# Storing only the read parts of a depthwise convolution, with its partitions regrouped as (q/k/v, chunk, channel), and loading the constants from GpSimd's queue

## The chip, the cores and the metric

The kernel runs on one core of one Trainium2 chip. The metric is the device time of one execution in microseconds (us). The kernel before was run three times: 3765.82, 3767.5 and 3774.27 us, median 3767.5 us.

## The reference

The input x is one image of 48 channels, 256 x 256, float32. Two layers are added to it in turn, each behind a group normalisation (16 groups of 3 channels):

```
x = x + L0(gn(x))        # attention between 4x4 patches
x = x + L1(gn(x))        # 64x64 windows: sum over 3 of (C, H, W) matrix products
```

Layer 0 is what the change touches. Its core is

```
qkv = depthwise3x3(einsum('bchw,oc->bohw', x, w_qkv))     # 144 channels = 3 x 8 heads x 6
q, k, v = heads(unfold(split(qkv, 3)))                    # per head 96 rows (6 channels x 16 pixels of a patch)
q, k = q / |q|, k / |k|                                   # over the 96 rows
out = v @ softmax(q^T k * temperature)                    # 8 heads, patches against patches
out = einsum(fold(out), w_proj)
```

There are 64 x 64 = 4096 patches inside the image (a border of zero patches is handled by a constant). The products of logits are made at nearly full float32 precision from two halves: q and k are split into a high part `oh` (float32r) and a low part `ol` (the difference), while v is used as it is.

## The kernel before, in words

The program has five stages that follow one another, each with its own loops.

**Statistics.** x is loaded into SBUF in ten parts of rows, the upper half of the image on SP's queue and the lower half on ScalarE's (L424), and VectorE makes statistics of each part (L428). Then come two tiny matmuls and the scaling of the weights `wq` and `wr` (L429 to L438). Before x, in program order, stand the constants: `gm`, `wq`, `wr`, `wp` and the temperatures `tb` are issued by ScalarE's queue (L86, L99, L103, L111), and the 21 pieces of the depthwise weights `dwt` by SP's (L109). The reductions of the temperatures (L115 to L120) end in `large`, an integer that says whether some temperature is so big that the softmax needs its row maxima.

**Pointwise, heads 0 and 1.** 64 products of the 1x1 convolution (L158), with results stored to DRAM in `t1` (L475).

**Depthwise, head 0** (`depthwise_first`, L365 to L406). A head's 18 channels (6 of q, 6 of k, 6 of v) are cut into 7 overlapping chunks of image rows, so that 126 partitions work at once. In the kernel before a partition is (chunk, q/k/v, channel). Ten steps r = 0 to 9 cover the rows of a chunk, four image rows at a time. Each step loads `pad` (L214 for the first two, L216 else), makes nine taps (on TensorE for even r and for r = 9, else on ScalarE and VectorE), squares and sums (L250, L254), norms with a matmul against `same` (L258), a scale (L284), and the split into `oh` (L293) and `ol` (L297). Then all 126 partitions of `o`, `oh` and `ol` are stored (L302) to `qkv[h]`, a DRAM tensor of [3 parts, 7 chunks, 18 x 16 rows, columns]. Of part 0 (`oh`) and part 1 (`ol`) only the rows of q and k are ever read, and of part 2 (`o`) only those of v. In head 0 SP stores `oh` and most `o`, and GpSimd most `ol`.

**Attention** (L521 to L715), under an order written out by hand. A branch on `large` (L487) stands before it. For each of 8 heads there are 16 steps g of two blocks of 128 queries: `scores` makes the logits (48 matmuls a step, L344) and exponentials (L563), `weigh` multiplies by the values (L592). Woven into head h are the depthwise rows of head h+1 (one a step, `rows[g]`), with `pad` loaded on SP's queue one step ahead (L700; for row 0 at the start of the head, L675) and stored on GpSimd's queue (L660, L689). Woven into head 0 alone are the 64 strips of the pointwise convolution of heads 2 to 7 (four a step): a load of x (L179), two products (L185), an eviction by ScalarE (L188), two stores (L197), all DMAs on SP's queue. SP issues in order, so its loads of keys, queries and values (L318) stand in one line with the strips and with `pad`.

**Projection and layer 1** (L719 to L916). The change does not touch these.

The order of the first three stages is a scheduler's: instructions are emitted in program order and moved ahead by priority where their waits allow it. In the stage of the head-0 depthwise only TensorE's order is fixed by hand.

Of the kernel before, what the change touches and what calls it, by code (L numbers as in the profile page):

```python
# [8 lines left out]
F32 = mybir.dt.float32  # L9
F32R = mybir.dt.float32r  # L10
AF = mybir.ActivationFunctionType
ALU = mybir.AluOpType
AX = mybir.AxisListType
# [7 lines left out]
KS = 4  # L21
KK = KS * KS
NH = 8
HD = C * KK // NH
# [3 lines left out]
TMAX = 60.0  # L28
CH = 7
CR = 9  # L30
HC = 3 * C // NH
NP1 = CH * HC
PX = W // KS
H0 = 2
M0 = H0 * HC
# [9 lines left out]
def conv_preact_kernel(  # L45
# [15 lines left out]
    nc = tc.nc  # L61
# [3 lines left out]
    const = ctx.enter_context(tc.tile_pool(name="const", bufs=1))  # L65
    dram = ctx.enter_context(tc.tile_pool(name="dram", bufs=1, space=DRAM))
# [5 lines left out]
    TR = 2 * CR * KS + (CH - 1) * CR * KS  # L72
    CN = CR * PX
    t1 = [dram.tile([(h1 - h0) * HC, TR, W + 2], F32, name=f"t1_{h0}") for h0, h1 in GROUPS]
    qkv = [dram.tile([3, CH, HC * KK, CN + PX], F32, name=f"qkv{h}") for h in range(NH)]

    os_ = dram.tile([NT // TP, C * KK, TP], F32, name="os_")
    x1s = dram.tile([C, H, W], F32, name="x1s")
# [3 lines left out]
    make_identity(nc, ident)  # L82
    ones = const.tile([C, 128], F32, name="ones")
    nc.vector.memset(ones, 1.0)
    gm = const.tile([P2, P2], F32, name="gm")
    nc.scalar.dma_start(out=gm, in_=gmat)  # L86

# [3 lines left out]
    wp = const.tile([P2, P2], F32, name="wp")  # L93
    nc.vector.memset(wp, 0.0)
    for s in range(2):
        r = slice(s * C, (s + 1) * C)
        for h in range(NH if s == 0 else H0):
            o = s * M0 + h * HC if h < H0 else (h - H0) * HC
            nc.scalar.dma_start(  # L99
                out=(wq[r] if h < H0 else wr[0:C])[:, o : o + HC].rearrange("c (z e) -> c z e", z=3),  # L100
                in_=w_qkvT.rearrange("c (z h e) -> h c z e", z=3, h=NH)[h],
            )
        nc.scalar.dma_start(out=wp[r, r], in_=w_projT)  # L103
    dwt = const.tile([NP1, NH, 9], F32, name="dwt")
    dws = w_dw.rearrange("(z h e) i a b -> z e h (i a b)", z=3, h=NH)
    for z in range(3):
        for j in range(CH):
            p = j * HC + z * 6
            nc.sync.dma_start(out=dwt[p : p + 6], in_=dws[z])  # L109
    tb = const.tile([1, NH], F32, name="tb")  # L110
    nc.scalar.dma_start(out=tb, in_=temp.rearrange("h a b -> (a b) h"))  # L111


    tabs = const.tile([1, 2], F32, name="tabs")
    nc.vector.tensor_reduce(tabs[:, 0:1], tb, AX.X, ALU.max)  # L115
    nc.vector.tensor_reduce(tabs[:, 1:2], tb, AX.X, ALU.min, negate=True)
    tlarge = const.tile([1, 1], F32, name="tlarge")
    nc.vector.tensor_reduce(tlarge, tabs, AX.X, ALU.max)
    large = const.tile([1, 1], mybir.dt.int32, name="large")
    nc.vector.tensor_single_scalar(large, tlarge, TMAX, ALU.is_gt)  # L120
    nmx = const.tile([128, NH * NT // 128], F32, name="nmx")
    nc.vector.memset(nmx, 0.0)

# [5 lines left out]

    same = const.tile([NP1, NP1], F32, name="same")  # L130

    nmul = const.tile([NP1, NH], F32, name="nmul")
    nadd = const.tile([NP1, 1], F32, name="nadd")

# [35 lines left out]
    class Strip:  # L170
# [5 lines left out]
        def load(self):  # L176
            self.xs = cv.tile([64 + C, 2, W], F32, name="xs", bufs=3)
            for s, rows in enumerate(both_halves(xc, 2 * self.j, 2)):
                nc.sync.dma_start(out=self.xs[s * 64 : s * 64 + C], in_=rows)  # L179
# [19 lines left out]
    class Depthwise:  # L199
# [3 lines left out]
            self.h, self.r = h, r  # L203
            self.pool, self.bufs = (pool, 4) if pool else (cv, 1)

        def load(self, engs=None):
            g = [i for i, (h0, h1) in enumerate(GROUPS) if h0 <= self.h < h1][0]
            c0 = (self.h - GROUPS[g][0]) * HC
            self.pad = self.pool.tile([NP1, KS + 2, W + 2], F32, name="pad", bufs=2 * self.bufs)
            rows = t1[g][c0 : c0 + HC, self.r * KS : self.r * KS + CH * CR * KS, :]  # L210
            rows = rows.rearrange("c (j y) x -> j c y x", j=CH)[:, :, : KS + 2, :]
            if engs:
                for j in range(CH):
                    engs[j % len(engs)].dma_start(out=self.pad[j * HC : (j + 1) * HC], in_=rows[j])  # L214
            else:
                nc.sync.dma_start(out=self.pad, in_=rows)  # L216

        def first(self):
            self.acc = self.pool.tile([NP1, KS, W], F32, name="acc", bufs=2)
            nc.scalar.mul(self.acc, self.pad[:, 0:KS, 0:W], dwt[:, self.h, 0:1])  # L220
# [31 lines left out]
        def reduce(self):  # L252
            self.ss = self.pool.tile([NP1, PX], F32, name="ss", bufs=self.bufs)
            nc.vector.tensor_reduce(self.ss, self.sq.rearrange("p a (x b) -> p x a b", b=KS), AX.XY, ALU.add)  # L254

        def norm(self):
            self.pn = one.tile([NP1, PX], F32, name="pn", tag="one")
            nc.tensor.matmul(self.pn, lhsT=same, rhs=self.ss, start=True, stop=True)  # L258

        def root(self, on_scalar=False):  # L260
            n = self.pool.tile([NP1, PX], F32, name="n", bufs=2)
            nc.vector.tensor_scalar_max(n, self.pn, 1e-24)
# [36 lines left out]
        def store(self, parts=(0, 1, 2), eng=nc.gpsimd):  # L299
            px = slice(self.r * PX, (self.r + 1) * PX)  # L300
            for i in parts:
                eng.dma_start(  # L302
                    out=qkv[self.h][i].rearrange("j (c k) n -> (j c) k n", k=KK)[:, :, px],
                    in_=self.o if i == 2 else (self.ol if i else self.oh).bitcast(F32),
                )


# [13 lines left out]

    def load_keys(kt, h, m, eng=nc.sync):
        col = m * 512, (m + 1) * 512
        k0, k1 = (qkv[h][i, :, HD : 2 * HD] for i in range(2))
        to = kt.bitcast(F32)
        load(to[0:HD, 0, :], k0, *col, eng)
        load(to[HD:128, 0, :], k1[:, 0:32], *col, eng)
        load(to[0:64, 1, :], k1[:, 32:], *col, eng)
        load(to[64:128, 1, :], k1[:, 32:], *col, eng)

    def load_queries(qt, h, g):
        col = g * 256, (g + 1) * 256
        to = qt.bitcast(F32)
        for i in range(2):
            qi = qkv[h][i, :, 0:HD]
            load(to[0:HD, i, :], qi, *col)
            load(to[HD:128, i, :], qi[:, 0:32], *col)
            load(to[i * 64 : (i + 1) * 64, 2, :], qi[:, 32:], *col)
# [70 lines left out]
    with tc.tile_pool(name="xn", bufs=1) as xnp, tc.tile_pool(name="cst", bufs=1) as cst, tc.tile_pool(  # L409
        name="nps", bufs=2, space=PSUM  # L410
# [9 lines left out]
        for i, LR in enumerate(parts):  # L420
            j = sum(parts[:i])
            for s in range(2):
                eng = nc.sync if s == 0 else nc.scalar
                eng.dma_start(  # L424
                    out=xr[s * C : (s + 1) * C, j : j + LR, :], in_=xc[:, s * HALF + j : s * HALF + j + LR, :]
# [8 lines left out]
        for g, (w, k) in enumerate(((wq, P2), (wr, C))):  # L434
            m = w.shape[1]
            pb = nps.tile([128, 1], F32, name="pb0", tag="pstat")
            nc.tensor.matmul(pb[:m], lhsT=w[:k], rhs=mean0[:k], start=True, stop=True)
            nc.vector.tensor_scalar_mul(bias[:m, g : g + 1], pb[:m], -1.0)  # L438

        pick = cst.tile([2 * CH, NP1], F32, name="pick")  # L440
        nc.vector.memset(pick, 0.0)
        nc.vector.tensor_copy(
            pick.rearrange("k (j z c) -> k j z c", j=CH, z=3)[:, :, 0:2],
            ident[: 2 * CH, : 2 * CH]
            .rearrange("k (j z u) -> k j z u", j=CH, u=1)
            .to_broadcast([2 * CH, CH, 2, 6]),
        )
        pk = nps.tile([NP1, NP1], F32, name="pk", bufs=1)
        nc.tensor.matmul(pk, lhsT=pick, rhs=pick, start=True, stop=True)
        nc.vector.tensor_copy(same, pk)  # L450
        row = cst.tile([1, NH + 1, NP1], F32, name="row")
        rv = row.rearrange("u i (j z c) -> u i j z c", j=CH, z=3)
        nc.vector.memset(row, 0.0)
        for i in range(NH):
            nc.vector.tensor_copy(
                rv[:, i, :, 0, :], tb[:, i : i + 1].rearrange("u (j c) -> u j c", j=1).to_broadcast([1, CH, 6])
            )
        nc.vector.memset(rv[:, :NH, :, 1, :], 1.0)
        nc.vector.memset(rv[:, NH, :, 2, :], 1.0)
        pr = nps.tile([NP1, NH + 1], F32, name="pr", bufs=1)  # L460
        for i in range(NH + 1):
            nc.tensor.matmul(pr[:, i : i + 1], lhsT=row[:, i, :], rhs=ones[0:1, 0:1], start=True, stop=True)
# [24 lines left out]
    with tc.If(nc.values_load(large) > 0):  # L487
# [8 lines left out]
        with tc.tile_pool(name="mk", bufs=NM) as mk, tc.tile_pool(name="mq", bufs=2) as mq, tc.tile_pool(  # L496
            name="mps", bufs=2, space=PSUM
        ) as mps:
            for h in range(NH):
# [5 lines left out]
                for nb in range(NB):  # L505
# [12 lines left out]
                    b = h * NB + nb  # L518
                    nc.vector.tensor_reduce(nmx[:, b : b + 1], mx, AX.X, ALU.max, negate=True)

    with tc.tile_pool(name="ahead", bufs=2) as ah, tc.tile_pool(name="ae", bufs=3) as ae, tc.tile_pool(  # L521
        name="asm", bufs=6
# [14 lines left out]
        def load_value(h, m):  # L537

            vt = ah.tile([HD, 4 * 128], F32, name="vt")
            load(vt, qkv[h][2, :, 2 * HD :], m * 512, (m + 1) * 512)  # L540
            values[h, m] = vt

        def turn(h, m):
# [88 lines left out]
        with tc.manual_schedule():  # L632
            load_query(0, 1)
            block = scores(0, 0)
            for h in range(NH):
                more = h + 1 < NH
                rows = {r: Depthwise(h + 1, r) for r in range(CR + 1)} if more else {}
                for g in range(NG):
                    p, d, n = rows.get(g - 2), rows.get(g - 1), rows.get(g)
# [82 lines left out]
    with tc.tile_pool(name="pj", bufs=3) as pj, tc.tile_pool(name="pjs", bufs=1) as pjs, tc.tile_pool(  # L722
        name="pps", bufs=3, space=PSUM
# [3 lines left out]
        for t in range(HALF // RP):  # L727
            ot = pj.tile([P2, KK, NP], F32, name="pot")
            xt = pj.tile([P2, RP, W], F32, name="pxt")
            for s in range(2):  # L730
                r = slice(s * C, (s + 1) * C)
# [38 lines left out]
        for s in range(2):  # L770
            nc.scalar.dma_start(
                out=csn[s * 64 : s * 64 + C].rearrange("c (t d) -> c t d", t=T3), in_=Cs.rearrange("t c d -> c t d")
            )
            r = slice(s * 64, s * 64 + C)
# [9 lines left out]
    with tc.tile_pool(name="lx", bufs=3) as lx, tc.tile_pool(name="lz", bufs=2) as lz, tc.tile_pool(  # L784
        name="lr", bufs=2
    ) as lr, tc.tile_pool(name="ly", bufs=4) as ly, tc.tile_pool(name="ps1", bufs=2, space=PSUM) as ps1, tc.tile_pool(
        name="ps2", bufs=2, space=PSUM
# [4 lines left out]
        for s in range(2):  # L792
            r = slice(s * WS, (s + 1) * WS)
# [164 lines left out]
```

## Time and profile before

| what | value |
|---|---|
| runs of the kernel, median (lowest to highest) | 3767.5 us (3765.82 to 3774.27) |
| profiled execution, its own time | 3774.41 us |
| span of the profile | 3772.6 us |
| PE busy / VectorE / ScalarE / GpSimd | 3521.1 / 2185.9 / 1715.5 / 597.5 us |
| largest groups: logits L344, values L592 | 1438.9 and 1423.5 us of PE |
| DMA moved | 441.64 MB, mean 117 GB/s |
| stores of the depthwise results (`qkv`) | 220 issues listed, 504.0 KB each |
| loads of `pad` | 78 issues listed, 761.9 KB each |

In the views of a profile, L12 is line 12 of the kernel, and a group is written as line, engine, operation, output<-input, shape and count. An engine's letter q (SPq, POOLq) is its sequencer, which issues DMAs: a line of SPq with a duration is time that SP spends in issuing. In a table of windows each engine has its busy time and, in brackets, its number of instructions; the last three columns are the granted TensorE clock, the mean busy share of the 16 DMA engines, and GB/s.

In time the stages lie as follows: statistics until 82 us, pointwise until 141 us, depthwise of head 0 with its stores until 286 us, the loading of the first keys until 310 us, attention until about 3320 us, and the rest until 3772.6 us.

### The profile page before, as it was taken

Reading aid. Unit: us, or ns where it says so; the run is one execution under the profiler, and the core shown is the slowest. Engines: PE = TensorE matmul, PEld = TensorE weight load, DVE = VectorE, ACT = ScalarE, POOL = GpSimd, SP = SyncE. Lnnn points to the kernel's source line nnn. Section 1 sums busy time; section 2 is a strip of 40 time slices with the busy share of each in tenths; the row PEclk is TensorE's granted clock in tenths of the full one; section 3 lists DMA queues with packets and bytes.
Section 4 is the critical chain, followed back from the end, with each engine's and each line's share of the span. In section 5 each row is a group of like instructions: output and inputs, shape, how many; then the busy total and the mean of one; then the engine's idle time right before and its main releaser. Section 6 shows DMA issues by size and latency. Waiting matters only on the chain.

```text
span 3772.6 us, 100069 instructions
## 1 busy us (share of the span) xinstructions
PE 3521.1 (93%) x44252; PEld 2916.8 (77%) x44252; DVE 2185.9 (58%) x3514; ACT 1715.5 (45%) x2667; POOL 597.5 (16%) x593
## 2 busy tenths in 40 slices
PE   1877999999999999999999999999999999955998
PEld 0335777788888888888888888888888888812776
DVE  5463675169727962896299439934992222256664
ACT  0224565555545554555455445545554444300222
POOL 0031121012301220122122112211221100010011
PEclk9988999999999999999999999999999999966999
DMA  6575666534433542354245424542543100199784
GB/s 144 170 172 159 178 192 177 166 111 118 114 83 99 126 113 73 104 125 107 84 106 122 101 77 113 119 104 75 125 114 93 46 19 23 31 242 199 128 145 91
DMA packets 307826, 441.64 MB, mean 117 GB/s; under 512 B 98474, under 2 KB 232954, under 8 KB 303160
## 3 DMA queue, kind: packets, MB, share of 16 engines
q1 hardware_dynamic: 253668, 269.65, 27.7%
q0 software_dynamic: 48320, 156.61, 18.5%
q10 hardware_dynamic: 5396, 8.88, 1.1%
q8 instruction: 351, 5.75, 0.7%
q14 instruction: 91, 0.75, 0.1%
HBM read 234.76 MB, written 199.95 MB: 115 GB/s over the span
## 4 chain that ended last, share of the span: by engine, by line
PE 84%; DMA 5%; issue 2%; ACT 0%; SPq 0%; DVE 0%; POOL 0%; ACTq 0%; POOLq 0%
PE big L344 37%; PE big L592 36%; PE pb L856 4%; PE pa L834 2%; PE pc L873 2%; PE big L185 2%; DMA x1s<-pxt 1%; DMA pxt<-in_x_dram 1%; DMA t<-ot 1%; PE pt L609 1%; PE pst L546 1%; PE pn L258 1%; DMA kt<-qkv 0%; DMA os__70<-oo 0%; DMA lxq<-x1s 0%
## 5 line engine op out<-in xcount | busy, mean ns | idle before, releaser
L563 ACT ACTIVATE e<-big,nmx 128x1024 f32<-128x1024 f32 x1024 | 1143.9, 1118 | 833.8 <-PE big L344 622.4
L344 PE MATMUL big<-kt,qt 128*128 128x512 f32 x6144 | 1438.9, 393 | 44.4 <-DMA qt<-qkv 31.6
L592 PEld LDWEIGHTS big<-vn,e 128*64 128x64 f32 x32768 | 1365.8, 137 | 83.4 <-ACT e L563 45.1
L592 PE MATMUL big<-vn,e 128*64 128x96 f32 x32768 | 1423.5, 247 | 5.0 <-ACT ot L188 3.1
L344 PEld LDWEIGHTS big<-kt,qt 128*128 128x128 f32 x6144 | 1145.1, 188 | 307.6 <-issue 46.2
L603 DVE TENSOR_TENSOR oacc<-big,oacc 128x768 f32<-128x768 f32 x480 | 458.1, 954 | 708.5 <-PE big L592 708.5
L239 DVE SCALAR_TENSOR_TENSOR acc<-pad,dwt,acc 126x1024 f32<-126x1024 f32 x592 | 766.2, 1295 | 39.1 <-ACT acc L220 23.5
L297 POOL TENSOR_TENSOR ol<-o,oh 126x1024 fp32r<-126x1024 f32 x78 | 187.1, 2399 | 925.3 <-DVE ss L254 800.9
L576 DVE TENSOR_REDUCE zt<-zs 128x1 f32<-128x4 f32 x256 | 38.9, 152 | 360.4 <-ACT e L563 360.4
L563 ACT ACTIVATION_READ_ACCUMULATOR e<-big,nmx 128x1 f32 x1024 | 196.2, 192 | 0.0
L841 DVE TENSOR_TENSOR lzt<-pa,cbias 128x864 f32<-128x864 f32 (+1 forms) x88 | 137.0, 1628 | 96.9 <-PE pa L834 96.9
L863 ACT COPY lyt<-pb 128x512 f32<-128x512 f32 x144 | 84.5, 586 | 212.9 <-PE pb L856 212.9
L302 POOL DMA_DIRECT2D qkv<-o x72 | 88.6, 1230 | 517.6 <-DVE zu L578 248.9
L613 POOL DMA_DIRECT2D os__70<-oo x128 | 65.2, 515 | 599.6 <-ACT oo L611 598.9
L250 ACT ACTIVATE sq<-acc 126x1024 f32<-126x1024 f32 x74 | 78.2, 1057 | 156.3 <-issue 111.1
L284 DVE TENSOR_TENSOR o<-acc,y 126x1024 f32<-126x1024 f32 x74 | 147.6, 1995 | 0.0
L856 PEld LDWEIGHTS pb<-wsb,lzt 128*64 128x64 f32 x2304 | 125.8, 138 | 27.6 <-issue 19.5
L856 PE MATMUL pb<-wsb,lzt 128*64 128x128 f32 x2304 | 141.7, 279 | 1.3 <-issue 1.3
L188 ACT ACTIVATE ot<-big,bias 108x1024 f32<-108x1024 f32 x64 | 71.1, 1112 | 153.7 <-PE big L185 81.4
L739 PE MATMUL pps<-pot,wp 96*96 96x512 f32 x128 | 78.2, 779 | 58.9 <-DMA pot<-os__70 58.9
L220 ACT ACTIVATE acc<-pad,dwt 126x1024 f32<-126x1024 f32 x74 | 84.1, 1137 | 83.0 <-DMA pad<-t 83.0
L318 POOL DMA_DIRECT2D kt<-qkv x44 | 22.9, 527 | 575.8 <-PE big L344 554.5
(116 smaller groups left out, 1904.5 us busy)
## 6 DMA issues: line engine op xcount, KB each, us to landing
pad<-t SPq DMA_DIRECT2D x78, 761.9 KB
qkv<-ol POOLq DMA_DIRECT2D x78, 504.0 KB, 8.9
qkv<-o POOLq DMA_DIRECT2D x72, 504.0 KB, 6.9
qkv<-oh POOLq DMA_DIRECT2D x70, 504.0 KB, 7.4
t<-ot SPq DMA_DIRECT2D x128, 217.7 KB
qt<-qkv SPq DMA_DIRECT2D x176, 96.0 KB
xs<-in_x_dram SPq DMA_DIRECT2D x128, 96.0 KB
os__70<-oo POOLq DMA_DIRECT2D x128, 96.0 KB, 2.1
```

The costliest lines, as they stand in the source:

```text
L220: nc.scalar.mul(self.acc, self.pad[:, 0:KS, 0:W], dwt[:, self.h, 0:1])
L239: nc.vector.scalar_tensor_tensor(self.acc, self.pad[:, dy : dy + KS, dx : dx + W], dwt[:, self.h, tap : tap + 1], self.acc, ALU.mult, ALU.add,
L284: nc.vector.tensor_tensor(self.o.rearrange("p (a b) x -> p a b x", a=KS), self.acc.rearrange("p a (x b) -> p a b x", b=KS), self.y.rearran ...
L297: eng.tensor_sub(self.ol, self.o, self.oh.bitcast(F32))
L302: eng.dma_start(out=qkv[self.h][i].rearrange("j (c k) n -> (j c) k n", k=KK)[:, :, px], in_=self.o if i == 2 else (self.ol if i else self. ...
L344: nc.tensor.matmul(ps[:, i, :], lhsT=qt[:, r, q0 : q0 + 128], rhs=kts[2 * j + i][:, r // 2, :], start=(r == 0), stop=(r == 2),)
L563: nc.scalar.activation(e[:, j * 1024 : (j + 1) * 1024], ps.rearrange("p a b -> p (a b)"), AF.Exp, bias=nmx[:, b : b + 1], accum_out=zs[:, ...
L592: nc.tensor.matmul(ps[p : p + 64, j // 4, j % 4 * HD : (j % 4 + 1) * HD], lhsT=e[:, mb * 128 + p : mb * 128 + p + 64], rhs=vn, start=(i == 0),
L603: nc.vector.tensor_add(oaccs[h, k], ps[:, :, : 4 * HD], oaccs[h, k])
L841: nc.vector.tensor_tensor(zv[:, :, y0 : y0 + n, :], pa[:, :, : n * T3 * C].rearrange("p s (y k) -> p s y k", y=n), cbias.rearrange("p (u v ...
L856: nc.tensor.matmul(pb[s * WS : (s + 1) * WS, i, :], lhsT=zts[u][:, t * C + c + i, :], rhs=wsb[:, t, :], start=True, stop=True,)
L863: nc.scalar.copy(yt[:, t, :], pb.rearrange("p i x -> p (i x)"))
```

## The change

Five edits:

1. A partition of the depthwise stage is now (q/k/v, chunk, channel): q fills partitions 0 to 41, k 42 to 83 and v 84 to 125. `dwt`, `pick` and `row` are laid out to match. `qkv[h]` becomes [3 parts, 3 (q, k, v), 7 chunks, 96 rows, columns], and the loads of keys, queries and values index it so; their lengths are the same.
2. `store` writes partitions 0 to 83 of `oh` and `ol`, and 84 to 125 of `o`, in place of all 126 of each.
3. `pad` is loaded with three DMAs of 42 partitions in place of one of 126 (or of seven of 18, for the first two rows of head 0).
4. All constants are issued from GpSimd's queue, the temperatures first. SP's and ScalarE's queues begin with x.
5. The reductions that end in `large` are moved in program order behind the statistics of x.

```diff
+NZ = NP1 // 3
...
-    qkv = [dram.tile([3, CH, HC * KK, CN + PX], F32, name=f"qkv{h}") for h in range(NH)]
+    qkv = [dram.tile([3, 3, CH, HD, CN + PX], F32, name=f"qkv{h}") for h in range(NH)]
...
+    tb = const.tile([1, NH], F32, name="tb")
+    nc.gpsimd.dma_start(out=tb, in_=temp.rearrange("h a b -> (a b) h"))
     gm = const.tile([P2, P2], F32, name="gm")
-    nc.scalar.dma_start(out=gm, in_=gmat)
+    nc.gpsimd.dma_start(out=gm, in_=gmat)
...
-            nc.scalar.dma_start(
+            nc.gpsimd.dma_start(
                 out=(wq[r] if h < H0 else wr[0:C])[:, o : o + HC].rearrange("c (z e) -> c z e", z=3),
                 in_=w_qkvT.rearrange("c (z h e) -> h c z e", z=3, h=NH)[h],
             )
-        nc.scalar.dma_start(out=wp[r, r], in_=w_projT)
+        nc.gpsimd.dma_start(out=wp[r, r], in_=w_projT)
...
     for z in range(3):
         for j in range(CH):
-            p = j * HC + z * 6
-            nc.sync.dma_start(out=dwt[p : p + 6], in_=dws[z])
-    tb = const.tile([1, NH], F32, name="tb")
-    nc.scalar.dma_start(out=tb, in_=temp.rearrange("h a b -> (a b) h"))
-
-
-    tabs = const.tile([1, 2], F32, name="tabs")
...
-    nc.vector.tensor_single_scalar(large, tlarge, TMAX, ALU.is_gt)
+            p = (z * CH + j) * 6
+            nc.gpsimd.dma_start(out=dwt[p : p + 6], in_=dws[z])
...
-        def load(self, engs=None):
+        def load(self, engs=(nc.sync,)):
...
-            rows = rows.rearrange("c (j y) x -> j c y x", j=CH)[:, :, : KS + 2, :]
-            if engs:
-                for j in range(CH):
-                    engs[j % len(engs)].dma_start(out=self.pad[j * HC : (j + 1) * HC], in_=rows[j])
-            else:
-                nc.sync.dma_start(out=self.pad, in_=rows)
+            rows = rows.rearrange("(z c) (j y) x -> z j c y x", z=3, j=CH)[:, :, :, : KS + 2, :]
+            for z in range(3):
+                engs[z % len(engs)].dma_start(out=self.pad[z * NZ : (z + 1) * NZ], in_=rows[z])
...
             for i in parts:
+                p = slice(2 * NZ, NP1) if i == 2 else slice(0, 2 * NZ)
                 eng.dma_start(
-                    out=qkv[self.h][i].rearrange("j (c k) n -> (j c) k n", k=KK)[:, :, px],
-                    in_=self.o if i == 2 else (self.ol if i else self.oh).bitcast(F32),
+                    out=qkv[self.h][i].rearrange("z j (c k) n -> (z j c) k n", k=KK)[p, :, px],
+                    in_=(self.o if i == 2 else (self.ol if i else self.oh).bitcast(F32))[p],
                 )
...
-        k0, k1 = (qkv[h][i, :, HD : 2 * HD] for i in range(2))
+        k0, k1 = (qkv[h][i, 1] for i in range(2))
...
-            qi = qkv[h][i, :, 0:HD]
+            qi = qkv[h][i, 0]
...
+        tabs = const.tile([1, 2], F32, name="tabs")
+        nc.vector.tensor_reduce(tabs[:, 0:1], tb, AX.X, ALU.max)
...
+        nc.vector.tensor_single_scalar(large, tlarge, TMAX, ALU.is_gt)
         pick = cst.tile([2 * CH, NP1], F32, name="pick")
...
-            pick.rearrange("k (j z c) -> k j z c", j=CH, z=3)[:, :, 0:2],
+            pick.rearrange("k (z j c) -> k z j c", j=CH, z=3)[:, 0:2],
...
-            load(vt, qkv[h][2, :, 2 * HD :], m * 512, (m + 1) * 512)
+            load(vt, qkv[h][2, 2], m * 512, (m + 1) * 512)
```

More of the change, by code (lines that the diff above doesn't have):

```diff
@@ L107, in conv_preact_kernel @@
         for j in range(CH):
-            p = j * HC + z * 6
-            nc.sync.dma_start(out=dwt[p : p + 6], in_=dws[z])
-    tb = const.tile([1, NH], F32, name="tb")
-    nc.scalar.dma_start(out=tb, in_=temp.rearrange("h a b -> (a b) h"))
-    tabs = const.tile([1, 2], F32, name="tabs")
[L115 to L119, printed above, removed]
-    nc.vector.tensor_single_scalar(large, tlarge, TMAX, ALU.is_gt)
+            p = (z * CH + j) * 6
+            nc.gpsimd.dma_start(out=dwt[p : p + 6], in_=dws[z])
     nmx = const.tile([128, NH * NT // 128], F32, name="nmx")
@@ L438, in conv_preact_kernel @@
             nc.vector.tensor_scalar_mul(bias[:m, g : g + 1], pb[:m], -1.0)
+        tabs = const.tile([1, 2], F32, name="tabs")
+        nc.vector.tensor_reduce(tabs[:, 0:1], tb, AX.X, ALU.max)
+        nc.vector.tensor_reduce(tabs[:, 1:2], tb, AX.X, ALU.min, negate=True)
+        tlarge = const.tile([1, 1], F32, name="tlarge")
+        nc.vector.tensor_reduce(tlarge, tabs, AX.X, ALU.max)
+        large = const.tile([1, 1], mybir.dt.int32, name="large")
+        nc.vector.tensor_single_scalar(large, tlarge, TMAX, ALU.is_gt)
         pick = cst.tile([2 * CH, NP1], F32, name="pick")
@@ L442, in conv_preact_kernel @@
         nc.vector.tensor_copy(
-            pick.rearrange("k (j z c) -> k j z c", j=CH, z=3)[:, :, 0:2],
+            pick.rearrange("k (z j c) -> k z j c", j=CH, z=3)[:, 0:2],
             ident[: 2 * CH, : 2 * CH]
-            .rearrange("k (j z u) -> k j z u", j=CH, u=1)
-            .to_broadcast([2 * CH, CH, 2, 6]),
+            .rearrange("k (z j u) -> k z j u", j=CH, u=1)
+            .to_broadcast([2 * CH, 2, CH, 6]),
         )
@@ L451, in conv_preact_kernel @@
         row = cst.tile([1, NH + 1, NP1], F32, name="row")
-        rv = row.rearrange("u i (j z c) -> u i j z c", j=CH, z=3)
+        rv = row.rearrange("u i (z j c) -> u i z j c", j=CH, z=3)
         nc.vector.memset(row, 0.0)
@@ L455, in conv_preact_kernel @@
             nc.vector.tensor_copy(
-                rv[:, i, :, 0, :], tb[:, i : i + 1].rearrange("u (j c) -> u j c", j=1).to_broadcast([1, CH, 6])
+                rv[:, i, 0], tb[:, i : i + 1].rearrange("u (j c) -> u j c", j=1).to_broadcast([1, CH, 6])
             )
-        nc.vector.memset(rv[:, :NH, :, 1, :], 1.0)
-        nc.vector.memset(rv[:, NH, :, 2, :], 1.0)
+        nc.vector.memset(rv[:, :NH, 1], 1.0)
+        nc.vector.memset(rv[:, NH, 2], 1.0)
         pr = nps.tile([NP1, NH + 1], F32, name="pr", bufs=1)
```

## The prediction, put on record before the changed kernel ran

> **What bounds the kernel now.** I read the windows of the whole span first. From 700 to 2700 us TensorE is busy 400.00 of every 400 us, so in heads 1 to 6 nothing that takes load off another engine can pay. What is left is the time before about 310 us, and head 0 of the attention (310 to 740 us). I then took the timeline of each of these stretches.
>
> The start, in the timeline (start, duration, engine, line, output<-input):
>
> ```profile
> 0.73 11.72 SPq L109 DMA_DIRECT2D dwt<-in_w_dw_dram  x21
> 9.82 12.67 ACTq L424 DMA_DIRECT2D xr<-in_x_dram  x6
> 15.65 9.63 SPq L424 DMA_DIRECT2D xr<-in_x_dram  x5
> 24.97 4.84 DVE L428 BATCH_NORM_STATS2 st<-xr 96x6 f32<-96x512 f32 x8 [9.66 <-DMA xr<-in_x_dram]
> ```
>
> x is first issued at 9.82 us by ScalarE and at 15.65 us by SP, because the constants stand ahead of it. VectorE needs 4.84 us for the statistics of a part that takes 7.2 us to arrive (it begins parts at 24.97, 31.02, 38.74, 46.39, 53.73, 61.10, 68.20), so the loading of x sets the end of this stage (77.8 us).
>
> The depthwise rows of head 0, in windows of 15 us (length, then busy time of PE, PEld, VectorE, ScalarE, GpSimd, then clock, DMA share, GB/s):
>
> ```profile
> 170.00:185.00 15.00, 15.00 (x37) 6.54 (x36) 14.71 (x13) 2.08 (x3) 0.00 (x0) 1.00 0.45 180
> 215.00:230.00 15.00, 15.00 (x39) 6.82 (x38) 14.82 (x13) 3.52 (x5) 7.81 (x4) 1.00 0.90 190
> 275.00:290.00 15.00, 0.00 (x0) 0.00 (x0) 0.00 (x0) 0.00 (x0) 3.21 (x7) 0.50 0.74 173
> ```
>
> TensorE is the limit until 257 us; then it runs dry, and from 266.3 us (the end of the last `ol`, L297) no engine works but the DMAs. SP's timeline shows what for:
>
> ```profile
> 273.39 2.51 SPq L302 DMA_DIRECT2D qkv<-ol  x1
> 276.00 2.31 SPq L302 DMA_DIRECT2D qkv<-oh  x1
> 278.39 2.48 SPq L302 DMA_DIRECT2D qkv<-ol  x1
> 286.71 3.03 SPq L318 DMA_DIRECT2D qt<-qkv  x6
> ```
>
> The last stores are issued until 280.87 us, the events of the branch (L487) on SP come at 285.5 to 286.1 us, and the first queries are loaded at 286.71 us. So a backlog of stores ends this stage.
>
> Head 0 of the attention, TensorE's timeline:
>
> ```profile
> 423.13 11.18 PE L344 MATMUL big<-kt,qt 128*128 128x512 f32 x48
> 439.84 0.58 PE L546 MATMUL pst<-ident,vt 96*128 96x96 f32 x4 [1.69 <-DMA vt<-qkv]
> 452.85 3.00 PE L185 MATMUL big<-xs,wr 48*108 48x512 f32 x4 [4.15 <-DMA xs<-in_x_dram]
> 462.75 11.17 PE L344 MATMUL big<-kt,qt 128*128 128x512 f32 x48
> ```
>
> An undisturbed step lasts 27.28 us (341.28, 368.56, 395.85, 423.13). This one lasts 39.62, that is 12.3 us more, waiting for loads. By the same reading the steps that begin at 570.93, 598.08 and 654.30 us lose 0.3, 2.0 and 4.0 us. All of head 0 loses 18.7 us to late DMAs, with a DMA share of 0.73 in the window from 390 to 420 us.
>
> **What the Trainium skill says.** The page "DMA: Bandwidth & Descriptors", section "Why a DMA increments its semaphore by 16 and not by 1", says that a DMA runs on the largest number of engines up to 16 that divides the slowest dimension of both sides. A `pad` load has 7 chunks outermost on one side and 126 partitions on the other, so 7 engines; the trace agrees (share 0.45 with only `pad` in flight, 7/16 = 0.44). A store of 126 partitions gets 14: 14/16 = 0.875, and the trace shows 0.88 to 0.90 while stores are queued. With 42 and 84 partitions the rule gives 7 and 14 again, so the change moves no work to fewer engines. The same page, section "Why small descriptors are slow (HBM only)", says that each small piece carries a fixed cost; the stores are pieces of 256 bytes, and the measured price below contains it. The same page, section "Queues, rings and completion order", says that an engine takes turns between queues, packet by packet. The trace has one hint for it: the first x load on SP waits until 15.65 us for a `dwt` piece issued between 10.05 and 12.4 us, beside x from ScalarE, so such a piece lands in 3.2 to 5.6 us and is not shut out.
>
> **The change part by part.** Sums are made against the profiled execution (3774.4 us, span 3772.6), which is 6.9 us above the median.
>
> *x ahead of the constants.* Both queues issue x at 0.73 us. The DMAs are saturated with x from about 11.5 to 70.9 us (share 0.96 to 1.1), 59.4 us for the whole. From 0.73 + 2 they would be done at 62.1 without the constants. The constants' pieces kept the DMAs busy some 0.3 of the first 9 us; I charge 2 us for mixing them in: 64.1 us. With both halves in step, the sixteen-row part that VectorE begins at 68.20 is there about one part (7.2 us) before the end, at 57, and the 9.6 us of statistics behind it follow: a gain of 11 us. If the two queues stay as uneven as now, only the 9.1 us of the earlier start less 2 are gained; if the constants cost nothing, 13. I take 11, ends 7 and 13.
>
> *Constants on GpSimd.* 36 issues, at 0.51 to 0.59 us each by its present ones (16 of `kt` in 8.19 us, 4 of `t` in 2.35). At most eight may be in flight, by the waits in the program order of the changed kernel; with 5.6 us to landing that is 0.7 us each, so 25 us. Behind them on GpSimd lie the zero borders of `t1` and the memsets of `ot0`, needed at 91 us today; `wq` is needed at 82, `dwt` at 148. All have 30 us of cover: cost nothing. The temperatures lead and their reductions, about 1 us of VectorE, and 4 us of tiny matmuls (L462) stand before the first statistics, done by 9 us, when the first x arrives at 10: nothing. If that cover failed by 3 us, VectorE's slack of 2.4 us a part would take it back.
>
> *Stores.* In the window from 200 to 260 us SP's queue shows 24,624 packets at 49.1% of 16 engines, so 471 us of engine time, 19.1 ns a piece. A store has 126 x 16 = 2016 pieces: 2016 x 19.1 / 14 = 2.75 us. Thirty stores are 82 us, and the stretch from the first to the last (194 to 286) is 92: the backlog. After: 20 stores of 1344 and 10 of 672 pieces, 33,600 x 19.1 / 14 = 46 us. A pair of rows costs 9.2 us of DMA every 18 us that TensorE needs, so nothing is left over when the last pair comes. Its first store can go at 262 us, its data are through at 271.5, and about 1.9 us later landed (today 285.5 less 280.87 less 2.75). Then the 1.2 us to the query load: 274.6 in place of 286.7, a gain of 12. What is late next is the pair itself: if 19.1 ns is also the price without a crowd it cannot be better by much (15, with pieces running as they come), and if the later `ol` is held up by SP's own issuing (2.3 us a store today, two thirds of it after), 8.
>
> *pad in three.* Same 7 engines, same pieces. The very first pads lose two engines (9 to 7, by the rule), but SP issues two pieces and not four ahead of the first row: 0, ends -1.5 and +1. Two more issues a row on SP, 0.81 us each today for a whole `pad`: in heads 1 to 6 they hide under TensorE, which stays at 400 of 400 although ScalarE has waited for `pad` at six starts of heads already, 49.4 us in sum. I take 0; if each start ran 1.6 us over its cover it would be 10 us lost.
>
> *Head 0.* Between 390 and 418 us GpSimd's stores take 25.8% of the engines. They shrink to 5/9, so 11.5% of the time falls away, 3.1 us a step. In the engines that carry `pad` (4.3 us a step by 25.7 GB/s each), the load goes from about 0.82 to 0.70. Four steps free 12.5 us ahead of the 12.3 us stall, and the later ones have two steps or more each. All 18.7 could go; but bursts remain, seven engines still carry `pad`, and SP has two more issues a row. I take two thirds, 12 us; ends +19 and -8 (ten rows at 0.8).
>
> Sum: 11 + 12 + 12 = 35 us of 3774.4; on the median 3767.5 x (1 - 35 / 3774.4) = 3732.6, say 3733.
>
> **The rivals.** *Head 0 keeps its stalls*: the late loads stand in SP's line, not in the engines' load. For it: SP spent 8.46 us on six query issues at 401.62, and 12.26 us on twelve at 431.64. Against it: those issues wait for DMAs eight places earlier that land 8 to 12 us late, as the engines are full. Gain 23: 3744.5. *Constants in the way of x*: with three queues taking turns, x loses what it gained, 11 us: 3744. Against it: their bytes are few. *The stores are not shortened*, since a DMA's fixed share and not its pieces counts: 3745. Against it: 30 x 2.75 us fits the stretch. *Slower*: SP's line in head 0 is full, and the extra `pad` issues push every load behind them. A `pad` issue took up to 2.38 us under pressure; two more at that price are 4.8 us a row, ten rows 48 us, against 23 from the start: 3792. It decides from 2.3 us a row that nothing covers. Against it: a third of a `pad` has a third of the pieces, and the stores lighten the same queues.
>
> **How the numbers follow.** Forecast 0.50; head 0 keeps its stalls 0.22; constants 0.11; stores 0.09; SP's line 0.08, of which 0.05 ends over 0.2% slower and 0.03 near the present time (0.2%, 7.5 us, is about what a measurement of this kernel can tell from no change). Faster 0.92, same 0.03, slower 0.05. The low end is all upper bounds, 13 + 15 + 19 = 47 us: 3720. The high end is the front and the drain at their low ends with nothing from head 0, 15 us: 3752.
>
> **What would show it.** Right: the first statistics near 10 us and rstd about 71 instead of 82; stores of head 0 landing 8 us after the last `ol`, not 19; steps of head 0 at 27.3 us throughout; DMA volume down by about 54 MB (80 rows x 1.333 x 0.516 = 55). Wrong: statistics waiting for temperatures or `wq`; a gap between `ol` and the query load as wide as before; new waits of ScalarE for `pad` in every head.

## The result and the profile after

The changed kernel takes 3743.39 us (median of 4 runs, 3735.86 to 3747.01) beside 3766.84 us for the kernel before (4 runs, 3765.82 to 3774.27). The medians differ by 23.5 us. The ratio on record is 0.9921, with a 95% interval of 0.9904 to 0.9937, which would be 30 us less; it is not the quotient of these two medians (0.9938), and the record does not say how it is formed. By either the gain is clear of zero. The forecast was 3733 us in a range of 3720 to 3752. The profiled execution took 3747.01 us, with a span of 3745.2 us.

Its start, in the timeline (start, duration, engine, line, output<-input):

```profile
0.72 26.32 SPq L414 DMA_DIRECT2D xr<-in_x_dram  x7
0.73 26.57 ACTq L414 DMA_DIRECT2D xr<-in_x_dram  x7
...
11.48 0.15 DVE L433 TENSOR_REDUCE tabs<-tb 1x1 f32<-1x8 f32 x1 [8.26 <-DMA tb<-in_temp_dram]
...
16.15 4.83 DVE L418 BATCH_NORM_STATS2 st<-xr 96x6 f32<-96x512 f32 x8
...
57.41 9.59 DVE L418 BATCH_NORM_STATS2 st<-xr 96x6 f32<-96x512 f32 x16 [2.81 <-DMA xr<-in_x_dram]
```

Both queues start x at once. The first statistics begin at 16.15 us, not near 10, because the temperatures are there only at 11.48 us and the tiny matmuls follow. Edit 5 does not show: although they stand behind the statistics in program order, the reductions of the temperatures (first line L433) still run ahead of them. The last sixteen rows begin at 57.41 us in place of 68.20, so the statistics end 10.8 us earlier in this pair of executions.

GpSimd in the same stretch, where the forecast had all constants through at 25 us:

```profile
1.30 0.69 POOL L87 DMA_DIRECT2D tb<-in_temp_dram  x1 [0.37 <-issue]
...
11.74 0.58 POOL L102 DMA_DIRECT2D wr<-in_w_qkvT_dram  x1 [5.37 <-DMA tb<-in_temp_dram]
16.72 0.58 POOL L102 DMA_DIRECT2D wr<-in_w_qkvT_dram  x1 [4.40 <-DMA gm<-in_gmat_dram]
...
59.59 0.57 POOL L112 DMA_DIRECT2D dwt<-in_w_dw_dram  x1 [1.11 <-DMA wp<-in_w_projT_dram]
61.34 0.57 POOL L112 DMA_DIRECT2D dwt<-in_w_dw_dram  x1 [1.19 <-DMA dwt<-in_w_dw_dram]
62.16 6.82 POOL L112 DMA_DIRECT2D dwt<-in_w_dw_dram  x12 [0.26 <-DMA dwt<-in_w_dw_dram]
```

The bracket names what each issue waited for: the ninth waits for the first, the tenth for the second. Beside x the first takes 10.4 us until its successor goes (1.30 to 11.74) and the second 14.4 (2.33 to 16.72, `gm`), so eight in flight move on slowly, and the last 12 follow at 0.57 us each about when x is through. The last of the 35 constants (I had counted 36) is issued at 69 us.

The end of the depthwise rows of head 0, SP's timeline:

```profile
256.28 1.41 SPq L292 DMA_DIRECT2D qkv<-oh  x1
257.79 2.42 SPq L292 DMA_DIRECT2D qkv<-ol  x1
265.40 3.04 SPq L308 DMA_DIRECT2D qt<-qkv  x6
```

The last `ol` is computed at 256.56 us and the first queries are loaded 8.8 us later (before: 266.34 and 286.71 us, 20.4 us).

Head 0 of the attention, TensorE's timeline:

```profile
402.62 11.18 PE L334 MATMUL big<-kt,qt 128*128 128x512 f32 x48
...
429.90 11.18 PE L334 MATMUL big<-kt,qt 128*128 128x512 f32 x48
...
457.18 11.18 PE L334 MATMUL big<-kt,qt 128*128 128x512 f32 x48
```

Steps are 27.28 us apart here, and no step of head 0 loses time. GpSimd's queue, which carries the stores, takes little more than half of the engines' time that it took, over 370 us of head 0 (packets, MB, share of 16 engines; the kernel before first, from 330 to 700 us, then the changed one from 310 to 680 us):

```profile
q0 software_dynamic: 4800, 15.52, 19.9%
```

```profile
q0 software_dynamic: 2880, 8.62, 11.7%
```

In the whole span the DMAs move 386.49 MB in place of 441.64, 55.15 MB less.

Since the same kernel's stages turned out to vary from one execution to the next, I use all profiles of both kernels (two of before, four of the changed one; each kernel was run again in the experiments below). Times are us from the span's start or lengths; a plus is time gained, mean against mean:

| stage | before | changed | gain |
|---|---|---|---|
| statistics end (aggregate starts) | 77.8, 78.2 | 67.0, 67.5, 69.1, 73.4 | +8.8 |
| from there to the first depthwise matmul | 77.5, 78.2 | 79.2, 79.7, 78.4, 80.1 | -1.5 |
| to the last `ol` | 111.0, 111.0 | 110.4, 110.4, 108.3, 110.7 | +1.1 |
| to the first query load | 20.4, 20.4 | 8.8, 9.6, 9.2, 9.1 | +11.2 |
| lost in head 0, over its undisturbed steps | 18.7, 10.7 | 0, 0, 1.3, 0 | +14.4 |
| first query load to the end of attention, without that loss | 3004.3, 3004.3 | 3003.4, 3002.4, 3002.4, 3002.9 | +1.5 |
| projection | 137.7, 145.1 | 148.1, 138.4, 141.5, 140.1 | -0.6 |
| rest | 316.7, 317.2 | 319.7, 318.3, 320.3, 315.6 | -1.5 |

(The 8.4 to 9.0 us between the attention's end and the projection are left out.) Up to the projection 35.4 us are gained, where the forecast had 35; in the first two profiles alone it was 40.9, of which 10.3 were given back in the projection.

### The profile page after: what moved, and what is told of

It reads as the page before. It is cut to its first block, busy times and chain, and to the rows that moved or that the text cites. A ratio compares the mean times of both kernels' runs of the same rounds, so it can differ in the third digit from the quotient of the medians.

```text
span 3745.2 us, 100375 instructions
## 1 busy us (share of the span) xinstructions
PE 3515.0 (94%) x44252; PEld 2913.5 (78%) x44252; DVE 2186.7 (58%) x3514; ACT 1717.9 (46%) x2667; POOL 548.3 (15%) x628
## 2 busy tenths in 40 slices
DMA packets 274147, 386.49 MB, mean 103 GB/s; under 512 B 77010, under 2 KB 211522, under 8 KB 269480
## 4 chain that ended last, share of the span: by engine, by line
PE 87%; DMA 4%; issue 1%; DVE 1%; SPq 0%; ACT 0%; POOL 0%; POOLq 0%; ACTq 0%; DVEq 0%
PE big L334 38%; PE big L591 37%; PE pb L855 4%; PE pa L833 2%; PE pc L872 2%; PE big L177 2%; DMA pxt<-in_x_dram 1%; PE pst L545 1%; PE pt L608 1%; DMA x1s<-pxt 1%; PE pn L247 1%; DMA pot<-os__70 1%; DMA kt<-qkv 0%; DVE pxt L745 0%; DMA lxq<-x1s 0%
## 5 line engine op out<-in xcount | busy, mean ns | idle before, releaser
L855 PEld LDWEIGHTS pb<-wsb,lzt 128*64 128x64 f32 x2304 | 126.2, 138 | 30.1 <-issue 21.9
L292 POOL DMA_DIRECT2D qkv<-o x72 | 56.3, 781 | 528.0 <-DVE zu L577 483.3
L738 PEld LDWEIGHTS pps<-pot,wp 96*96 96x96 f32 x128 | 26.6, 216 | 120.6 <-issue 117.5
```

The costliest lines, as they stand in the source:

```text
L738: nc.tensor.matmul(ps[:, i : i + 2, :], lhsT=wp, rhs=ot[:, ki * KS + i : ki * KS + i + 2, :], start=True, stop=True,)
L855: nc.tensor.matmul(pb[s * WS : (s + 1) * WS, i, :], lhsT=zts[u][:, t * C + c + i, :], rhs=wsb[:, t, :], start=True, stop=True,)
```

## The experiments

The first group asked which edits the gain comes from. Its kernels ran on one chip, where the kernel before took 3772.18 us (35 runs, 3762.27 to 3785.8).

**after_again: the changed kernel once more.** No edit.

> The changed kernel unchanged, for how its projection and layer 1 come out in another execution. In the first profile of it the gain stood at 40 us when the projection began, and 27 us at the end: the projection took 148.1 us from its first matmul to the end of its statistics, against 137.7 before. Theory (the loss is variation between executions of a stage that is all DMA): the projection lasts anywhere from 137 to 148 us here, and the stages before it keep their gains of 11, 11 and 19 us. Rival (the change itself slows the projection, for instance by where its tensors lie): 147 to 149 us again, and so in every kernel with the new layout of the stored parts.

Measured: 3742.28 us (6 runs), ratio 0.991 [0.989, 0.993]. The projection took 138.4 us, where the first profile has 148.1. From 3290 to 3390 us of that stage the DMA share is 1, and only the rate differs. The windows of the first profile (length, busy time of PE, PEld, VectorE, ScalarE, GpSimd, clock, DMA share, GB/s):

```profile
3310.00:3330.00 20.00, 9.21 (x16) 3.07 (x16) 12.35 (x12) 0.00 (x0) 1.01 (x2) 0.67 1.01 231
3330.00:3350.00 20.00, 9.10 (x16) 3.16 (x16) 12.33 (x12) 0.00 (x0) 1.01 (x2) 0.67 1.02 243
```

The same windows in after_again:

```profile
3310.00:3330.00 20.00, 9.13 (x16) 3.16 (x16) 12.50 (x13) 0.00 (x0) 1.01 (x2) 0.67 1.01 261
3330.00:3350.00 20.00, 13.13 (x20) 4.53 (x21) 12.45 (x12) 0.00 (x0) 1.01 (x2) 0.67 1.00 270
```

The share is 1 in both, and one program moves 231 or 261 GB/s. So the 10 us given back are not a cost of the change: the rival, that the new layout slows the projection, fell. Three kernels further down with the same projection, all on one chip, show the same spread: 141.4 us in after_third, 148.2 in pad_six and 139.9 in dwt_behind_x. What sets the rate in an execution stays open.

**parts_only: edits 1 to 3 alone.** The constants go back to ScalarE's and SP's queues and the reductions to their old place:

```diff
-    nc.gpsimd.dma_start(out=gm, in_=gmat)
+    nc.scalar.dma_start(out=gm, in_=gmat)
...
-            nc.gpsimd.dma_start(out=dwt[p : p + 6], in_=dws[z])
+            nc.sync.dma_start(out=dwt[p : p + 6], in_=dws[z])
```

> Edits 1 to 3 alone (partitions regrouped, only the read parts stored, pad in three DMAs); the constants stay on the queues of SP and ScalarE. Theory (the gains of the stages are independent): statistics end near 78 us as before, the gap between the last low part and the first query load is 8 to 9 us and not 20, the steps of head 0 all last 26.8 to 27.5 us; 3767 - 12 - 19 = 3736 us, up to 3747 with a slow projection. Rival (head 0 gained from the earlier start or from constants on GpSimd): steps of 30 us and more come back, 3750.

Measured: 3747.18 us (6 runs), ratio 0.9917 [0.9896, 0.9938]; statistics end at 77.4 us as before, 8.9 us from the last `ol` to the queries, no loss in head 0. Edits 1 to 3 alone bring the drain and head 0. (The expected 3736 to 3747 us were counted from 3767; on this chip the kernel before takes 3772.18.)

**constants_only: edits 4 and 5 alone**, on the kernel before.

> Edits 4 and 5 alone (all constants on GpSimd's queue, temperatures first, their reductions behind the statistics of x); all three parts are stored in full and pad is one DMA. Theory: statistics end near 67 us, the drain of the stores is as long as before (20 us from the last low part to the query load), head 0 loses some 19 us again; 3767 - 10 = 3757 us. Rival (the constants also free SP's queue for head 0): below 3750.

Measured: 3764.68 us (22 runs), ratio 0.9977 [0.9966, 0.9987]; statistics end at 69.6 us, the drain is 20.9 us as before, and head 0 loses 8.4 us, less than half of the 19 expected. The time is 7.7 us above the expected 3757; against the kernel before on this chip it is 7.5 us less, where 10 were expected. TensorE's timeline has two waits for `xs` in its step at 444 us:

```profile
444.97 1.08 PE L178 MATMUL big<-xs,wr 48*108 48x512 f32 x2 [2.60 <-DMA xs<-in_x_dram]
447.28 1.82 PE L178 MATMUL big<-xs,wr 48*108 48x512 f32 x2 [1.23 <-DMA xs<-in_x_dram]
```

The ratios multiply to 0.9917 x 0.9977 = 0.9894, which the intervals do not tell from the changed kernel's 0.991: within them the two halves add.

**all_parts: everything but edit 2.** All 126 partitions are stored again, with the new grouping and `pad` in three:

```diff
-                p = slice(2 * NZ, NP1) if i == 2 else slice(0, 2 * NZ)
+                p = slice(0, NP1)
```

> The changed kernel with edit 2 undone: all 126 partitions of the three parts are stored; the partitions, the three DMAs of pad and the constants stay changed. Theory (the fewer stored pieces make both the shorter drain and the smooth head 0): the gap before the query load is 20 us again and head 0 loses 15 to 25 us again; 3757 us. Rival (pad in three DMAs smooths head 0): only the drain comes back, steps of 27 us in head 0, 3750. Second rival (three DMAs of pad cost something that the fewer stores hide): 3765 or more.

Measured: 3772.51 us (14 runs), ratio 0.9992 [0.9976, 1.0008]. The drain is back (24.5 us), and so are head 0's stalls (14.2 us in steps of 31.1, 28.9 and 35.6 us), of which one line, as before:

```profile
449.31 1.50 PE L177 MATMUL big<-xs,wr 48*108 48x512 f32 x4 [3.39 <-DMA xs<-in_x_dram]
```

So it is the storing of fewer parts, not the splitting of `pad`, that cures head 0. The time is above the expected 3757 and where the second rival had it (3765 or more): with full stores, regrouping and three pads cost 7.8 us more than constants_only by the medians. The intervals of the two ratios overlap, so this is not firm. In the profiles 3.6 us of it are in the drain and 5.8 in head 0, whose loss varies between executions. That the fewer stores hide a cost of the three pads is thus not excluded; what the changed kernel itself shows is the 1.5 us before the first depthwise matmul.

The second group asked after the stalls, SP's issuing and the constants (the kernel before on that chip: 3774.8 us, 9 runs).

**before_again: the kernel before once more**, a single execution.

> The kernel before, unchanged, for a second profile of it. Theory (the 18.7 us that its head 0 loses are a steady loss of a stage whose DMAs are near their limit, not an accident of one execution): 12 to 30 us lost over the steps of head 0, in whichever steps; gap from the last low part to the first query load 19 to 22 us; projection anywhere from 137 to 149 us. Rival (the first profile was an unlucky execution): less than 6 us lost in head 0.

Measured: 3775.88 us. Head 0 loses 10.7 us in steps of 34.8, 29.0 and 29.0 us, just short of the 12 that were expected at least. TensorE's timeline:

```profile
442.04 0.78 PE L546 MATMUL pst<-ident,vt 96*128 96x96 f32 x4 [2.66 <-DMA vt<-qkv]
...
453.66 1.33 PE L185 MATMUL big<-xs,wr 48*108 48x512 f32 x4 [2.81 <-DMA xs<-in_x_dram]
```

The stalls belong to the kernel before, in the same place with another size. All four profiles with full stores lose 8.4 to 18.7 us, and all eight with fewer lose 0 to 1.3.

**after_third: the changed kernel a third time.**

> The changed kernel unchanged, on the same chip as the next two, as their base. Steps of head 0 without loss, gap 8.5 to 10 us, 0.990 to 0.993 of the time before.

Measured: 3738.61 us (4 runs), ratio 0.9902 [0.9886, 0.9919]; projection 141.5 us, head 0 loses 1.3 us.

**pad_six: six DMAs a `pad` in place of three**, to double SP's issues for it:

```diff
             for z in range(3):
-                engs[z % len(engs)].dma_start(out=self.pad[z * NZ : (z + 1) * NZ], in_=rows[z])
+                for y in (0, 3):
+                    engs[z % len(engs)].dma_start(
+                        out=self.pad[z * NZ : (z + 1) * NZ, y : y + 3], in_=rows[z][:, :, y : y + 3, :]
+                    )
```

> The changed kernel with each of the three DMAs of pad cut into two of three image rows: six issues a row on SP's queue, the same engines and bytes, twice the pieces of half the size. It doubles the suspected cost of the three DMAs. Theory (with fewer stored pieces the queues have room, and the issues are covered): steps of head 0 still within 1 us of 27.3 us, time within 5 us of the changed kernel. Rival (SP's line in head 0 is nearly full, and the three DMAs already used its room): 10 us or more lost in head 0 and 10 us in the time.

Measured: 3743.41 us (4 runs), ratio 0.9907 [0.9891, 0.9923]; no loss in head 0. SP's timeline at the start of the attention, pad_six:

```profile
305.08 4.97 SPq L206 DMA_DIRECT2D pad<-t  x6
```

and the changed kernel:

```profile
303.42 3.08 SPq L205 DMA_DIRECT2D pad<-t  x3
```

Three more issues cost SP 1.9 us. Head 0 begins about 4 us later, and after that nothing is lost: even three issues more a row than the change has left TensorE's steps as they were, so the slower rival fell.

**dwt_behind_x: the depthwise weights issued by SP and ScalarE behind x**, to see whether the constants slow x:

```diff
-            nc.gpsimd.dma_start(out=dwt[p : p + 6], in_=dws[z])
...
+                (nc.sync, nc.scalar)[j % 2].dma_start(out=dwt[p : p + 6], in_=dws[z])
```

> The changed kernel with the 21 pieces of the depthwise weights issued by SP and ScalarE behind x, in place of GpSimd beside x. Theory (the pieces of the constants are few, x is limited by its own bytes): the parts of x arrive at the same pace, statistics begin their last sixteen rows within 1.5 us of the changed kernel on this chip, same time within 4 us; GpSimd is through with its constants before 45 us and not at 69. Rival (constants beside x slow it): the last part 3 us or more earlier.

Measured: 3741.18 us (5 runs), ratio 0.9912 [0.9899, 0.9926]. GpSimd has issued its last constant at 35.4 us. But the last part of x begins at 62.91 us, later than in after_third, not earlier. VectorE's timeline in dwt_behind_x:

```profile
62.91 9.59 DVE L414 BATCH_NORM_STATS2 st<-xr 96x6 f32<-96x512 f32 x16 [3.18 <-DMA xr<-in_x_dram]
```

and in after_third:

```profile
59.43 9.59 DVE L418 BATCH_NORM_STATS2 st<-xr 96x6 f32<-96x512 f32 x16 [3.27 <-DMA xr<-in_x_dram]
```

Neither expectation held: x came 3.5 us later, outside the theory's 1.5, and the rival had the sign wrong. From 20 to 60 us x arrives here at 186 GB/s and in after_third at 202. The third group went on with this.

**constants_behind_x: all constants but the temperatures behind x**, on the chip of after_fourth (the kernel before there: 3773.25 us, 11 runs). The 34 constants other than the temperatures are spread over the two queues:

```diff
+        for i, (o, a) in enumerate(late):
+            (nc.sync, nc.scalar)[i % 2].dma_start(out=o, in_=a)
         group_stats(st0, mean0, rstd0, cst, nps)
```

> The changed kernel, with every constant but the temperatures issued by SP and ScalarE behind their loads of x instead of by GpSimd beside them (nothing left out). It asks what has slowed the arrival of x from 7.2 us a part in the kernel before to about 7.6 us and more in the changed one. Theory A (the constants on GpSimd's queue cost x nothing; the pace varies from execution to execution): x's aggregate starts within 67 to 71 us, as in the profiles of the changed kernel so far, and the time is within 0.2% of it; the 12 weights, the mask and the 21 dwt pieces then land behind x, and if they hold the scaling of the weights up, the first pointwise product comes up to 5 us later. Theory B (constants beside x take 3 us and more from it): parts are 7.2 us apart again and the aggregate starts at 64 to 66 us.

Measured: 3742.79 us (6 runs), ratio 0.9926 [0.9913, 0.9939]; the aggregate starts at 69.6 us, as Theory A has it, and x arrives at 206 GB/s from 20 to 60 us.

**after_fourth: the changed kernel, its base.**

> The changed kernel once more, on the same chip, as the base for the comparison: aggregate at 67 to 71 us, no stalls in head 0 over 2 us, time 3733 to 3748 us; the projection stage anywhere between 138 and 148 us if its length varies between executions.

Measured: 3742.4 us (6 runs), ratio 0.9922 [0.9909, 0.9936]. The aggregate starts at 73.4 us, outside the 67 to 71 that I expected. Here is the reason, in one window of the first profile of the changed kernel:

```profile
20.00:60.00 40.00, 0.00 (x0) 0.00 (x0) 27.88 (x48) 1.28 (x1) 6.66 (x12) 1.00 1.00 212
```

and of after_fourth:

```profile
20.00:60.00 40.00, 0.00 (x0) 0.00 (x0) 26.48 (x45) 1.28 (x1) 5.10 (x9) 1.00 1.02 190
```

The DMA share is 1 and the program is the same, but x arrives at 212 or 190 GB/s. The kernel before has 202 and 198 here. Theory B's 64 to 66 us did not come. On this chip the kernel with the constants beside x is 3.8 us later than the one with them behind it, but the same start varies as much on one chip: after_again, constants_only and all_parts load x at 210, 201 and 189 GB/s. The constants cost x nothing that can be told from this; a cost of a few us is not excluded by one profile.

## Why the prediction was right, step by step

| step | forecast | measured (mean against mean) |
|---|---|---|
| x ahead of the constants | 11 (7 to 13) | 8.8 (10.8 in the first profiles) |
| first pads | 0 (-1.5 to +1) | -1.5 |
| drain of the stores | 12 (8 to 15) | 11.2, and 1.1 before it |
| head 0 | 12 (-8 to +19) | 14.4 |
| heads 1 to 6, the rest | 0 | -0.6 (1.5 - 0.6 - 1.5) |
| sum | 35 | 33.4; spans differ by 33.5 |

- **x.** The mechanism held: x is issued at 0.73 us, and the stage ends earlier. In the first profile the DMA share is about 1 from 4 us on and falls to 0.54 in the window from 60 to 62 us, so x is through at about 61; in the other three it is through at about 62, 64 and 68. The mean is the 64 that I had. The term that was mis-sized is "about one part (7.2 us) before the end, at 57": the last sixteen-row part begins at 57.41, 57.83, 59.43 and 63.76 us, about 4 us before x is through and not 7.2, in the mean at 59.6. That accounts for the 2 us that are missing from the 11. The rate does not explain it: from 20 to 60 us the four have 212, 210, 202 and 190 GB/s, about 203 in the mean, and the kernel before 202 and 198. In the first profile the high rate made up for the wrong step, which was luck.
- **The step that failed: "such a piece lands in 3.2 to 5.6 us", "with 5.6 us to landing that is 0.7 us each, so 25 us", and the temperatures' matmuls "done by 9 us".** The temperatures take 10 us from issue to use, the constants last until 69 us, and the first statistics begin at 16.2. The landing time was misread in the trace of before. What SP's first load of x waits for until 15.65 us is the first load of x on ScalarE's queue (issued at 9.82), no piece of `dwt`. SP's third load of x, at 20.37 us, does wait for such a piece, one of the last six, issued between 10.05 and 12.11 us: it landed after 8 to 10 us. SP's waits in the kernel before (us in total, times, longest), from 12.5 to 15.9 us and from 17.4 to 20.5 us:

```profile
SPq L424 <- DMA xr<-in_x_dram: 3.2, 1, 3.2
```

```profile
SPq L424 <- DMA dwt<-in_w_dw_dram: 3.0, 1, 3.0
```

So the trace of before already had the 10 us. The error cost nothing. VectorE needs 4.8 us for a part that comes every 7.6 us, the slack that the prediction had named: it does the second part without a wait (21.09 us) and waits for x again from the third. On GpSimd the memsets of `ot0`, for which I had 30 us of cover and more, end at 69.6 us, and the first store of `ot0` goes at 80.5 us: 11 us are left. The zero borders follow until 71.8 us and are first read with `pad` at 137.7. That so wrong a duration found enough cover was luck.

- **Drain.** 19.1 ns a piece was about the right price (18.2 on GpSimd's queue in the changed kernel, see the end), and the backlog is gone: from 218 to 224 us, between two pairs of rows, the DMA share is 0.00. The query load comes 8.8 to 9.6 us after the last `ol`, where the sum had 8.3 (274.6 less 266.3). The Trainium skill's rule for the number of engines ("DMA: Bandwidth & Descriptors", section "Why a DMA increments its semaphore by 16 and not by 1"), by which stores of 84 and of 42 partitions keep 14 engines and a `pad` load of 42 keeps 7, was not contradicted; these runs do not measure a single store's engines.
- **pad in three.** The first depthwise matmul comes 1.5 us later after the statistics, the low end that I gave for two engines fewer. TensorE's wait for `pad` before it makes most of this: 13.8 and 14.1 us before, 15.0 to 15.3 in the changed kernel, 14.3 in constants_only with the old loads. That the two engines are the reason is not shown. Within the steps SP's issues are hidden, as pad_six shows with twice the number.
- **Head 0.** All of the stalls went, not "two thirds", but there was less to gain: the 18.7 us of the first profile was the worse of the two of before, 14.7 in the mean. The two errors cancel, so the closeness of 12 and 14.4 is partly luck. That the cause is the stores is shown by all_parts; whether it is their share of the engines or the order in which loads get their turn was not separated.
- **The rivals.** Head 0 did not keep its stalls (eight profiles); the constants did not take the 11 us back from x; the stores were shortened; SP's line was not full. The time is 10 us above the forecast all the same. By the medians of the four comparisons the gain is 23.5, 29.9, 36.2 and 30.9 us (3766.84 less 3743.39, 3772.18 less 3742.28, 3774.8 less 3738.61, 3773.25 less 3742.4); the result is the smallest of them, and both kernels spread over some 10 us and more, with what their projection, head 0 and x cost in an execution. The four give 30.1 in the mean, so my 35 was some 5 us too much by this measure and 1.6 by the spans of the profiles; more cannot be told from these runs.

## What to carry to other kernels

Count what a store writes against what is read: lining the unread part up along partitions let a slice drop it, and where stores are backlogged at the end of a stage, the gain was the backlog that no longer stood behind the last piece (12 us forecast, 11.2 measured), not all of the DMA time saved (26,880 pieces x 19.1 ns / 14, about 37 us), and a second one where the same traffic delayed loads under a busy TensorE. Constants may be issued on another queue beside a large load, but reckon their landing at what the trace shows beside such a load (10 us and more here, eight in flight), make sure which DMA a wait is for before taking a duration from it, and check the last user of that queue, not only the first. Before a few us in a stage that only waits for DMAs are put down to a change, profile the same kernel twice.

## What the runs showed of the hardware

- With a DMA share of 1, the rate of one program's stage differs between executions: 190 to 212 GB/s while x is loaded, and 138.4 to 148.1 us for the projection. These profiles of the changed kernel lie on at least three chips; on one chip, kernels with the same code for the stage differ as much (189 to 210 GB/s, 139.9 to 148.2 us).
- Small loads on GpSimd's queue beside two full queues of x land late: the temperatures (32 bytes) were used 10.2 us after their issue, and the second and third loads released their successors after 14.4 and 17.1 us (2.91 to 20.02); with x gone, issues follow every 0.57 us. On SP's queue in the kernel before, a piece of `dwt` beside x took 8 to 10 us.
- 256-byte pieces cost 18 to 20 ns of an engine each: 19.1 ns on SP's queue before. On GpSimd's queue the listing packs them into packets of 3 KB; counted by 256 bytes, 2.76 MB from 190 to 250 us in the changed kernel took 20.4% of 16 engines, 196 us for 10,780 pieces, 18.2 ns. The same count in the kernel before (3.99 MB and 33.1% from 200 to 260 us) gives 20.4 ns.
